# A recurrence's weights prepared in larger pieces, their transfers issued by GpSimd

## The chip, the core and the metric

The kernel runs on one core of one Trainium2 chip, in one launch. The metric is the time of one execution on the device, in microseconds (us), as the median of several runs. Engines are named as in the profile: PE is TensorE (PEld its weight loads), DVE is VectorE, ACT is ScalarE, POOL is GpSimd, SP is SyncE, which here only issues transfers (DMAs). SPq, ACTq and POOLq are these engines' own instruction queues, in which a DMA is issued or a semaphore waited for.

## What is computed

The reference takes 32 batch elements of 512 nodes with 256 channels and a 512 x 512 adjacency for each. Two layers follow each other, each with a graph part and a sequence part:

```python
x = x + gnn0(layernorm(x), adj)      # graph attention of 4 heads, relu, layernorm of each head
x = x + mamba2(layernorm(x))         # gated state-space block over the 512 nodes
x = x + gnn1(layernorm(x), adj)      # graph attention of one head, elu
x = x + lstm_part(layernorm(x))      # below
```

The last part is a recurrence that runs over the 512 nodes one after the other, for all 32 elements at once, so it can only begin when the last element has left gnn1:

```python
gates = x_proj + h @ W_hh.T                     # x_proj = x @ W_ih.T + b_ih + b_hh
i, f, g, o = split(gates, 4)
c = sigmoid(f) * c + sigmoid(i) * tanh(g)
h = sigmoid(o) * tanh(c)
```

Its hidden states are then weighted by an argmax of two logits, summed along the nodes, and combined with two vectors fw_att and bw_att. The weights of this part (W_ih, W_hh, the biases, the logit weights, fw_att, bw_att) are what the change is about. They are inputs, each used once.

## The kernel before, in words

The program has two phases. In the first, `layers_per_batch` takes the elements one after the other through gnn0, mamba2 and gnn1. Four streams of generators run at staggered times: while element b is in `mamba`, element b+2 is in gnn0 (`plain0`, then `after0`) and element b-1 is in gnn1 (`plain1`, `after1`). A loop always takes the next step of the stream whose planned time is lowest (lines 1005 to 1019); that is the order of recording. A scheduler then orders the instructions on each engine, and every engine executes its own queue strictly in order. An instruction that has to wait stops everything behind it on that engine.

A fifth stream, recorded in the last two elements (planned times from nb - 1.75 on, line 1014), is `recurrence_weights`. It reads the recurrence's weights from memory, scales and reorders their columns on GpSimd and stores the result in a DRAM tensor `wr`. The second phase, `recurrence`, begins by loading `wr` into the tile `wall` (line 1283).

The pieces of `recurrence_weights` that matter here:

- `begun` (L1078) writes a column of a tile with a copy from the current element's x. It ties the preparation to that element's place in the work. The DMA that fills the tile comes after that copy.
- The small inputs come first: eight loads for the logit weights `rwl` (L1088), the biases (L1095, L1098), and fw and bw in four loads each (L1111), with stores at L1104, L1106 and L1115.
- W_ih is taken in eight quarters of 128 x 256 (two halves k of the input channels, four quarters q): a load of the quarter into `rwraw` (L1123; two buffers, by q), a load of one row repeated on all partitions into `rwoff` (L1125), a subtraction (L1132), `ordered` (a memset of two columns, L1069, and four products, L1075) into `rwt`, and a store to `wr` (L1140). For the second half k the store has 127 rows, since the last row is another one's place (L1139).
- W_hh follows in eight quarters, each with four loads of 32 rows (L1129), `ordered`, one product of a single column (L1135) and a store.
- The pool of these tiles has one buffer for each tag. So `rwt` is used by all pieces in turn: its next memset waits until the store before has been done.
- SyncE issues all of these DMAs.

Around it, the lines that the prediction names: the store of an element's result X3 (L879, SyncE, once for each element), the broadcast loads of mamba's decay rows `bc` (L753) and `ce` (L675), of the attention's rows `rb` and `rbv` (L465), all on SyncE; `line` and `linea` to DRAM from ScalarE (L661, L452); on GpSimd the additions L494 and L605, the small pair L54/L56 (a reciprocal square root for the layer norms and for mamba's norm), the product `ce` (L746), the bias of gnn0's output `o` (L593), mamba's `xdd` (L793) and `xh` (L817). VectorE's L341 continues `o` after L593; its L783 makes `xdt`, which L793 reads, and TensorE's L780 and L800 stand before and behind it in mamba.

Of the kernel before, what the change touches and what calls it, by code (L numbers as in the profile page):

```python
# [14 lines left out]
ALU = mybir.AluOpType  # L15
# [4 lines left out]
P = 128  # L20
N = 512
NT = N // P
D = 256
DK = D // P
# [9 lines left out]
GB = 32  # L34
# [41 lines left out]
def layers_per_batch(ctx, tc, c, a, X3, odd=None, wr=None):  # L76
# [6 lines left out]
    nc = tc.nc  # L83
    nb = a.x.shape[0]
# [917 lines left out]
    def each(*parts):  # L1002
        return stream([(b + at, b + until, make, b + n) for b in range(-2, nb + 1) for at, until, make, n in parts])

    streams = [
        each((0.0, 1.0, mamba, 0)),
        each((-0.097, -0.033, mamba_in, 0), (-0.026, 0.192, mamba_dt, 0)),
        each((0.55, 0.857, second, -1), (0.857, 1.52, first, 2)),
        each((1.62, 1.75, after0, 2)),
    ]  # L1010
    if odd is not None:
        rw = ctx.enter_context(tc.tile_pool(name="rw0", bufs=1))
        now = lambda: states[int(min(at))]["x"][:, 0, 0:1]
        streams.append(nb - 1.75 + 1.5 / 64 * n for n, _ in enumerate(recurrence_weights(nc, rw, a, wr, now)))
    END = nb + 10
    at = [next(t) for t in streams]
    while min(at) < END:
        n = at.index(min(at))
        at[n] = next(streams[n], END)

    if odd is not None:
# [12 lines left out]
        for most, n in ((mall0, H0), (mall1, 1)):  # L1034
            pair = wp.tile([4 * n, n], F32, name=f"pair{n}")
# [12 lines left out]
def recurrence_weights(nc, pool, a, wr, now):  # L1048

    Q, J = 4, 64
    W = 4 * J + 2
    nw = DK * Q * W
    n0 = 2 * nw  # L1060
    half = (0.5, 0.5, 0.5, 1.0)
    order = (3, 1, 0, 2)

    def tile_(p, n, tag):
        return pool.tile([p, n], F32, tag=tag, name=tag)

    def ordered(raw, n, s):
        t = tile_(P, W, "rwt")
        nc.gpsimd.memset(t[:n, 4 * J :], 0.0)  # L1069
        halves = t[:n, : 3 * J].rearrange("p (e g j) -> p e g j", e=2, g=3)  # L1070
        for to, g in enumerate(order):
            dst, src = t[:n, 3 * J : 4 * J], raw[:n, g * J : (g + 1) * J]
            if to < 3:
                dst, src = halves[:, :, to, :], src.rearrange("p (e j) -> p e j", e=2)
            nc.gpsimd.tensor_scalar(dst, src, half[g] * s, None, ALU.mult)  # L1075
        return t

    def begun(t, *columns):  # L1078
        for n in columns or (0,):
            nc.gpsimd.tensor_copy(t[:, n : n + 1], now())  # L1080
        return t

    yield

    wl = begun(tile_(P, 2 * DK, "rwl"), 0, DK)
    for q in range(Q):
        for l in range(2):
            nc.sync.dma_start(  # L1088
                out=wl[q * 32 : (q + 1) * 32, l * DK : (l + 1) * DK],
                in_=a.wl[q : q + 1, l * J : (l + 1) * J].rearrange("o (k p) -> p (o k)", p=32),  # L1090
            )
    yield
    nc.gpsimd.tensor_tensor(wl[:, :DK], wl[:, DK:], wl[:, :DK], ALU.subtract)
    bl = begun(tile_(P, 2, "rbl"))
    nc.sync.dma_start(out=bl, in_=a.bl.to_broadcast([P, 2]))  # L1095
    b = [begun(tile_(P, 4 * J, f"rwraw{n}")) for n in range(2)]
    for t, src in zip(b, (a.bih, a.bhh)):
        nc.sync.dma_start(out=t[:Q], in_=src.rearrange("o (q r) -> (o q) r", q=Q))  # L1098
    yield
    nc.gpsimd.tensor_tensor(bl[:, 0:1], bl[:, 0:1], bl[:, 1:2], ALU.subtract)  # L1100
    nc.gpsimd.tensor_tensor(b[0][:Q], b[0][:Q], b[1][:Q], ALU.add)
    t = ordered(b[0], Q, 1.0)
    yield
    nc.sync.dma_start(out=wr[:, n0 + 2 * J : n0 + 2 * J + 1], in_=bl[:, 0:1])  # L1104
    last = wr[P - 1 : P, nw - Q * W : nw].rearrange("o (q w) -> (o q) w", q=Q)
    nc.sync.dma_start(out=last, in_=t[:Q])  # L1106
    yield
    for n, src in enumerate((a.fw, a.bw)):
        t = begun(tile_(P, W, "rwt"))
        for q in range(Q):  # L1110
            nc.sync.dma_start(out=t[q * GB : (q + 1) * GB, :J], in_=src[q : q + 1, :].to_broadcast([GB, J]))  # L1111
        yield
        nc.gpsimd.tensor_scalar(t[:, :J], t[:, :J], 0.5, None, ALU.mult)
        yield
        nc.sync.dma_start(out=wr[:, n0 + n * J : n0 + (n + 1) * J], in_=t[:, :J])  # L1115
        yield
    for n, (src, s) in enumerate(((a.wih, 1.0), (a.whh, 0.5))):
        for k in range(DK):
            for q in range(Q):
                raw = begun(tile_(P, 4 * J, f"rwraw{q % 2}"))  # L1120
                cols = slice(q * 4 * J, (q + 1) * 4 * J)
                if n == 0:
                    nc.sync.dma_start(out=raw, in_=src[k * P : (k + 1) * P, cols])  # L1123
                    off = begun(tile_(P, 4 * J, "rwoff"))
                    nc.sync.dma_start(out=off, in_=src[D - 1 : D, cols].to_broadcast([P, 4 * J]))  # L1125
                else:
                    for r in range(Q):
                        r0 = r * J + k * 32
                        nc.sync.dma_start(out=raw[r * 32 : (r + 1) * 32], in_=src[r0 : r0 + 32, cols])  # L1129
                yield  # L1130
                if n == 0:
                    nc.gpsimd.tensor_tensor(raw, raw, off, ALU.subtract)  # L1132
                t = ordered(raw, P, s)
                if n == 1:
                    nc.gpsimd.tensor_scalar(t[:, 4 * J : 4 * J + 1], wl[:, k : k + 1], 0.5, None, ALU.mult)  # L1135
                yield
                o0 = n * nw + (k * Q + q) * W

                r = P - 1 if n == 0 and k == DK - 1 else P  # L1139
                nc.sync.dma_start(out=wr[:r, o0 : o0 + W], in_=t[:r])  # L1140
                yield


def recurrence(ctx, tc, c, a, X3, wr, out):
# [247 lines left out]
@with_exitstack  # L1392
def kernel(ctx: ExitStack, tc: tile.TileContext, a, out):
    nc = tc.nc
    nb = a.x.shape[0]
    const = ctx.enter_context(tc.tile_pool(name="const", bufs=1))
    dram = ctx.enter_context(tc.tile_pool(name="dram", bufs=1, space=DRAM))
    c = setup_consts(nc, const)
    X3 = dram.tile([N, nb, D], F32, name="X3")
    wr = dram.tile([P, 2 * DK * 4 * 258 + 2 * 64 + 1], F32, name="wr")  # L1400
    odd = const.tile([1, 1], I32, name="odd")
    with ExitStack() as phase:
        layers_per_batch(phase, tc, c, a, X3, odd, wr)
    general = nc.values_load(odd, min_val=0, max_val=1, skip_runtime_bounds_check_because="it is only compared with 0")
    with tc.If(general > 0):
        with ExitStack() as phase:
            layers_per_batch(phase, tc, c, a, X3)
    with ExitStack() as phase:
        recurrence(phase, tc, c, a, X3, wr, out)
# [70 lines left out]
```

## Time and profile before

| | |
|---|---|
| median of 3 runs | 4534.08 us (4533.77 to 4534.99) |
| the profiled execution: its time | 4532.62 us |
| the profiled execution: its span | 4530.9 us |
| PE, DVE, ACT, POOL busy, of the span | 86%, 74%, 65%, 28% |
| first phase: last X3 store issued | 3211.65 us |
| second phase: `wall` loads issued | from 3220.98 us |
| DMAs issued by SyncE: packets, bytes | 269832, 271.32 MB |
| DMAs issued by GpSimd: packets, bytes | 160, 0.04 MB |
| weights: first copy on GpSimd, last store issued | 2948.65 us, 3135.90 us |

The profile is that of one execution, whose span runs from its first to its last instruction. The timelines give start and duration in us, engine, line, operation, output and input, the count (x4: four instructions in a row), and in brackets the idle time before the row with what ended it. In the table of stretches each row has the stretch and its length, then for PE, PEld, DVE, ACT and POOL the busy time and in parentheses the number of instructions, then the granted TensorE clock as a share of full speed, the busy share of the DMA engines and the GB/s moved. In the list of waits, "A <- B: total, times, longest" says that A was idle until B let it go.

### The profile page before, as it was taken

How to read it: one execution, taken by the hardware profiler on the slowest of the kernel's cores; microseconds unless marked ns; L12 is line 12 of the kernel's file. 1: busy time of each engine (PE TensorE's matmuls, PEld its weight loads, DVE VectorE, ACT ScalarE, POOL GpSimd, SP SyncE). 2: the span in 40 equal slices, each digit the busy share in tenths (PEclk: the TensorE clock that was granted, in tenths of full speed). 3: DMA queues.
4: the chain of work that ended last, by engine and by line, in shares of the span. 5: the costliest groups of instructions: out<-in, count | busy, mean ns of one | idle time of the engine just before them, and what ended most of it. 6: DMA issues, size and time to landing. Idle time of an engine off the chain costs nothing. (4 is left out here: it accounts for less than half of the span.)

```text
span 4530.9 us, 116255 instructions
## 1 busy us (share of the span) xinstructions
PE 3878.2 (86%) x46798; PEld 2389.2 (53%) x46798; DVE 3375.1 (74%) x10429; ACT 2956.8 (65%) x6852; POOL 1286.6 (28%) x1371
## 2 busy tenths in 40 slices
PE   6889999988999989998999999867688888888883
PEld 3445554455544455444555444534466666666662
DVE  4677676777667776677767677744599999999997
ACT  4677777777777777777777777755344444444441
POOL 2334433334333344333343333443000000000000
PEclk8999999999999999999999999988899999999997
DMA  3111222112221212222122211122112221222225
GB/s 107 56 61 59 75 66 73 61 64 69 72 73 61 64 57 75 71 70 64 59 71 70 73 61 64 57 68 60 52 41 46 46 46 42 45 46 46 46 41 170
DMA packets 273755, 288.69 MB, mean 64 GB/s; under 512 B 151872, under 2 KB 224536, under 8 KB 271032
## 3 DMA queue, kind: packets, MB, share of 16 engines
q1 hardware_dynamic: 269832, 271.32, 20.8%
q10 hardware_dynamic: 3216, 9.81, 0.7%
q8 instruction: 371, 6.08, 0.5%
q14 instruction: 176, 1.44, 0.1%
q0 software_dynamic: 160, 0.04, 0.0%
HBM read 227.09 MB, written 37.11 MB: 58 GB/s over the span
## 5 line engine op out<-in xcount | busy, mean ns | idle before, releaser
L1267 PE MATMUL pg<-wall,h 128*32 128x96 f32 x16352 | 558.4, 276 | 177.4 <-DVE h L1349 169.8
L1267 PEld LDWEIGHTS pg<-wall,h 128*32 128x32 f32 x16352 | 374.2, 109 | 351.0 <-DVE h L1349 332.8
L1267 PE MATMUL pg<-wall,xTr 128*32 128x96 f32 (+1 forms) x16384 | 548.3, 273 | 0.0
L484 DVE SCALAR_TENSOR_TENSOR w<-w,adjT 128x1024 f32<-128x1024 f32 x256 | 348.0, 1380 | 247.6 <-ACT w L478 247.6
L1267 PEld LDWEIGHTS pg<-wall,xTr 128*32 128x32 f32 x16384 | 447.3, 110 | 4.7 <-issue 0.3
L1326 ACT ACTIVATE z<-pg 128x96 f32<-128x96 f32 x512 | 128.7, 251 | 438.6 <-PE pg L1267 438.6
L710 DVE SCALAR_TENSOR_TENSOR acc<-px,convw,acc 128x511 f32<-128x511 f32 (+2 forms) x480 | 351.2, 743 | 83.1 <-ACT acc L705 75.3
L478 ACT ACTIVATE w<-rb,neg,colsa 128x512 f32<-128x512 f32 x512 | 387.5, 807 | 8.7 <-PE psu L556 4.4
L746 POOL TENSOR_TENSOR ce<-ce,cT 128x384 f32<-128x384 f32 x128 | 185.3, 1476 | 654.4 <-ACT cT L718 650.7
L548 PE MATMUL pav<-w,hb 128*64 128x512 f32 x1024 | 350.3, 610 | 7.4 <-DVE w L484 4.4
L1337 ACT ACTIVATE z<-z 128x32 f32<-128x32 f32 x1024 | 234.7, 229 | 168.4 <-DVE z L1335 101.0
L760 ACT ACTIVATE g<-bc,cs 128x128 f32<-128x128 f32 x1024 | 321.6, 389 | 7.3 <-DMA bc<-line 4.9
L54 POOL TENSOR_SCALAR ve<-mv 128x4 f32<-128x4 f32 x32 | 6.3, 196 | 1064.2 <-DVE mv L1191 1064.2
L689 PE MATMUL px<-mT,win 128*128 128x512 f32 x640 | 307.1, 611 | 0.0
L962 PE MATMUL pov<-wb,wv 128*128 128x257 f32 x1024 | 241.2, 388 | 72.2 <-DVE wv L484 72.2
L847 PE MATMUL po<-wc,xh 128*128 128x256 f32 x1024 | 259.4, 388 | 44.5 <-DVE xh L817 28.7
L56 POOL TENSOR_TENSOR rs<-ve,mhalf 128x4 f32<-128x4 f32 (+1 forms) x224 | 276.7, 1235 | 18.4
L962 PEld LDWEIGHTS pov<-wb,wv 128*128 128x128 f32 x1024 | 190.6, 191 | 115.8 <-DVE wv L484 87.0
L1349 DVE STREAM_TRANSPOSE h<-hh 128x32 f32<-128x32 f32 x1024 | 216.6, 212 | 34.9
L689 PE MATMUL pz<-mT,win 128*128 128x512 f32 x512 | 242.2, 606 | 0.0
L1332 DVE SCALAR_TENSOR_TENSOR ab<-z 128x64 f32<-128x64 f32 x1024 | 226.3, 221 | 14.5 <-ACT z L1326 11.2
L847 PEld LDWEIGHTS po<-wc,xh 128*128 128x128 f32 x1024 | 181.7, 192 | 88.1 <-DVE xh L817 41.3
(249 smaller groups left out, 8419.5 us busy)
## 6 DMA issues: line engine op xcount, KB each, us to landing
bc<-line SPq DMA_DIRECT2D x128, 512.0 KB, 3.6
adj<-in_adj_dram SPq DMA_DIRECT2D x32, 1024.0 KB
rb<-linea SPq DMA_DIRECT2D x64, 512.0 KB, 4.9
ce<-line SPq DMA_DIRECT2D x64, 384.0 KB, 4.5
x<-in_x_dram SPq DMA_DIRECT2D x32, 512.0 KB, 8.7
X<-x SPq DMA_DIRECT2D x32, 512.0 KB
xt<-X SPq DMA_DIRECT2D x128, 128.0 KB, 2.1
x<-X SPq DMA_DIRECT2D x128, 128.0 KB, 3.4
```

Of the source, the lines that this page charges most:

```text
L56: nc.gpsimd.tensor_tensor(rs, ve, c.mhalf[:, :n], ALU.pow)
L478: nc.scalar.activation(w[:, t, k, :], rb[:, k, :], AF.Relu, bias=neg1, scale=cols[:, 2 * m + t, h + k : h + k + 1],)
L484: nc.vector.scalar_tensor_tensor(w[:, :, k, :], w[:, :, k, :], 1.0, edges, ALU.add, ALU.mult)
L548: nc.tensor.matmul(pa[k * HO : (k + 1) * HO, :], hb[:, j, 2 * q + k, :], w[:, t, k, :], start=(j == 0), stop=(j == NT - 1),)
L689: nc.tensor.matmul(pz, win[:, k, col : col + P], mT[:, k, :], start=(k == 0), stop=(k == DK - 1))
L710: nc.vector.scalar_tensor_tensor(acc[:, s:], pz[:, : N - s], convw[:, cc, k : k + 1], acc[:, s:], ALU.mult, ALU.add)
L760: nc.scalar.activation(g[:, i, k, :], bc[:, k, i * P : (i + 1) * P], AF.Relu, bias=cs[:, i, 2 * cc + k : 2 * cc + k + 1], scale=-1.0,)
L847: nc.tensor.matmul(po[:, i * D : (i + 1) * D], xh[:, cc, it * P : (it + 1) * P], wc[:, cc, :], start=(cc == 0), stop=(cc == NC - 1),)
L962: nc.tensor.matmul(po[:, : D + 1], ws[j // 2][:, j % 2, 0, it * P : (it + 1) * P], wb[:, j, :], start=(j == 0), stop=(j == NT - 1),)
L1267: nc.tensor.matmul(p[q * GB : (q + 1) * GB, :], lhs[k], w[:, k, q, s:e], start=(start and k == 0), stop=(stop and k == DK - 1),)
L1332: nc.vector.scalar_tensor_tensor(ab, z[:, c0 + 2 * H : c0 + 4 * H], 1.0, z[:, c0 : c0 + 2 * H], ALU.add, ALU.mult)
L1337: nc.scalar.activation(z[:, (10 + n) * H : (11 + n) * H], z2[:, 4 * n * H : (4 * n + 1) * H], AF.Tanh, scale=0.5)
```

## The change

Three things change in `recurrence_weights`, and one in its pacing.

All its DMAs are issued by GpSimd, none by SyncE. `rwoff` is gone: the quarter of W_ih and the repeated row share one tile `rwraw` of 512 columns, which has a single buffer. W_ih is taken with q as the outer and k as the inner loop. W_hh is taken in four pieces of two quarters, with four loads of 32 x 512 and one store of 128 x 516 each. fw and bw share one tile, one product and one store. `ordered` takes one or two quarters; its three first products are split in two, each over 32 columns of each quarter. The planned times are spread over 48 steps where they were spread over 64 before.

```diff
--- before.py
+++ after.py
@@ -1011,7 +1011,7 @@
     if odd is not None:
         rw = ctx.enter_context(tc.tile_pool(name="rw0", bufs=1))
         now = lambda: states[int(min(at))]["x"][:, 0, 0:1]
-        streams.append(nb - 1.75 + 1.5 / 64 * n for n, _ in enumerate(recurrence_weights(nc, rw, a, wr, now)))
+        streams.append(nb - 1.75 + 1.5 / 48 * n for n, _ in enumerate(recurrence_weights(nc, rw, a, wr, now)))
     END = nb + 10
     at = [next(t) for t in streams]
     while min(at) < END:
@@ -1064,16 +1064,23 @@
     def tile_(p, n, tag):
         return pool.tile([p, n], F32, tag=tag, name=tag)
 
-    def ordered(raw, n, s):
-        t = tile_(P, W, "rwt")
-        nc.gpsimd.memset(t[:n, 4 * J :], 0.0)
-        halves = t[:n, : 3 * J].rearrange("p (e g j) -> p e g j", e=2, g=3)
+    def ordered(raw, n, quarters, s):
+
+        t = tile_(P, 2 * W, "rwt")
+        tq = t.rearrange("p (q w) -> p q w", q=2)[:n, :quarters]
+        rq = raw.rearrange("p (q w) -> p q w", q=quarters)[:n]
+        nc.gpsimd.memset(tq[:, :, 4 * J :], 0.0)
         for to, g in enumerate(order):
-            dst, src = t[:n, 3 * J : 4 * J], raw[:n, g * J : (g + 1) * J]
+            src = rq[:, :, g * J : (g + 1) * J]
             if to < 3:
-                dst, src = halves[:, :, to, :], src.rearrange("p (e j) -> p e j", e=2)
-            nc.gpsimd.tensor_scalar(dst, src, half[g] * s, None, ALU.mult)
-        return t
+                for e in range(2):
+                    nc.gpsimd.tensor_scalar(
+                        tq[:, :, (3 * e + to) * 32 : (3 * e + to + 1) * 32], src[:, :, e * 32 : (e + 1) * 32],
+                        half[g] * s, None, ALU.mult,
+                    )
+            else:
+                nc.gpsimd.tensor_scalar(tq[:, :, 3 * J : 4 * J], src, half[g] * s, None, ALU.mult)
+        return t, tq
 
     def begun(t, *columns):
         for n in columns or (0,):
@@ -1083,62 +1090,69 @@
     yield
 
     wl = begun(tile_(P, 2 * DK, "rwl"), 0, DK)
-    for q in range(Q):
-        for l in range(2):
-            nc.sync.dma_start(
+    for l in range(2):
+        for q in range(Q):
+            nc.gpsimd.dma_start(
                 out=wl[q * 32 : (q + 1) * 32, l * DK : (l + 1) * DK],
                 in_=a.wl[q : q + 1, l * J : (l + 1) * J].rearrange("o (k p) -> p (o k)", p=32),
             )
-    yield
+        yield
     nc.gpsimd.tensor_tensor(wl[:, :DK], wl[:, DK:], wl[:, :DK], ALU.subtract)
     bl = begun(tile_(P, 2, "rbl"))
-    nc.sync.dma_start(out=bl, in_=a.bl.to_broadcast([P, 2]))
-    b = [begun(tile_(P, 4 * J, f"rwraw{n}")) for n in range(2)]
+    nc.gpsimd.dma_start(out=bl, in_=a.bl.to_broadcast([P, 2]))
+    both = begun(tile_(P, 2 * 4 * J, "rwraw"), 0, 4 * J)
+    b = [both[:, : 4 * J], both[:, 4 * J :]]
     for t, src in zip(b, (a.bih, a.bhh)):
-        nc.sync.dma_start(out=t[:Q], in_=src.rearrange("o (q r) -> (o q) r", q=Q))
+        nc.gpsimd.dma_start(out=t[:Q], in_=src.rearrange("o (q r) -> (o q) r", q=Q))
     yield
     nc.gpsimd.tensor_tensor(bl[:, 0:1], bl[:, 0:1], bl[:, 1:2], ALU.subtract)
     nc.gpsimd.tensor_tensor(b[0][:Q], b[0][:Q], b[1][:Q], ALU.add)
-    t = ordered(b[0], Q, 1.0)
+    t, _ = ordered(b[0], Q, 1, 1.0)
     yield
-    nc.sync.dma_start(out=wr[:, n0 + 2 * J : n0 + 2 * J + 1], in_=bl[:, 0:1])
+    nc.gpsimd.dma_start(out=wr[:, n0 + 2 * J : n0 + 2 * J + 1], in_=bl[:, 0:1])
     last = wr[P - 1 : P, nw - Q * W : nw].rearrange("o (q w) -> (o q) w", q=Q)
-    nc.sync.dma_start(out=last, in_=t[:Q])
+    nc.gpsimd.dma_start(out=last, in_=t[:Q, :W])
     yield
+    t = begun(tile_(P, 2 * W, "rwt"))
     for n, src in enumerate((a.fw, a.bw)):
-        t = begun(tile_(P, W, "rwt"))
         for q in range(Q):
-            nc.sync.dma_start(out=t[q * GB : (q + 1) * GB, :J], in_=src[q : q + 1, :].to_broadcast([GB, J]))
-        yield
-        nc.gpsimd.tensor_scalar(t[:, :J], t[:, :J], 0.5, None, ALU.mult)
-        yield
-        nc.sync.dma_start(out=wr[:, n0 + n * J : n0 + (n + 1) * J], in_=t[:, :J])
-        yield
-    for n, (src, s) in enumerate(((a.wih, 1.0), (a.whh, 0.5))):
+            nc.gpsimd.dma_start(out=t[q * GB : (q + 1) * GB, n * J : (n + 1) * J], in_=src[q : q + 1, :].to_broadcast([GB, J]))
+        yield
+    nc.gpsimd.tensor_scalar(t[:, : 2 * J], t[:, : 2 * J], 0.5, None, ALU.mult)
+    yield
+    nc.gpsimd.dma_start(out=wr[:, n0 : n0 + 2 * J], in_=t[:, : 2 * J])
+    yield
+
+    for q in range(Q):
+        cols = slice(q * 4 * J, (q + 1) * 4 * J)
         for k in range(DK):
-            for q in range(Q):
-                raw = begun(tile_(P, 4 * J, f"rwraw{q % 2}"))
-                cols = slice(q * 4 * J, (q + 1) * 4 * J)
-                if n == 0:
-                    nc.sync.dma_start(out=raw, in_=src[k * P : (k + 1) * P, cols])
-                    off = begun(tile_(P, 4 * J, "rwoff"))
-                    nc.sync.dma_start(out=off, in_=src[D - 1 : D, cols].to_broadcast([P, 4 * J]))
-                else:
-                    for r in range(Q):
-                        r0 = r * J + k * 32
-                        nc.sync.dma_start(out=raw[r * 32 : (r + 1) * 32], in_=src[r0 : r0 + 32, cols])
-                yield
-                if n == 0:
-                    nc.gpsimd.tensor_tensor(raw, raw, off, ALU.subtract)
-                t = ordered(raw, P, s)
-                if n == 1:
-                    nc.gpsimd.tensor_scalar(t[:, 4 * J : 4 * J + 1], wl[:, k : k + 1], 0.5, None, ALU.mult)
-                yield
-                o0 = n * nw + (k * Q + q) * W
-
-                r = P - 1 if n == 0 and k == DK - 1 else P
-                nc.sync.dma_start(out=wr[:r, o0 : o0 + W], in_=t[:r])
-                yield
+            pair = begun(tile_(P, 2 * 4 * J, "rwraw"), 0, 4 * J)
+            raw, off = pair[:, : 4 * J], pair[:, 4 * J :]
+            nc.gpsimd.dma_start(out=raw, in_=a.wih[k * P : (k + 1) * P, cols])
+            nc.gpsimd.dma_start(out=off, in_=a.wih[D - 1 : D, cols].to_broadcast([P, 4 * J]))
+            yield
+            nc.gpsimd.tensor_tensor(raw, raw, off, ALU.subtract)
+            t, _ = ordered(raw, P, 1, 1.0)
+            yield
+            o0 = (k * Q + q) * W
+
+            r = P if k < DK - 1 else P - 1
+            nc.gpsimd.dma_start(out=wr[:r, o0 : o0 + W], in_=t[:r, :W])
+            yield
+    for q in (0, 2):
+        for k in range(DK):
+            raw = begun(tile_(P, 2 * 4 * J, "rwraw"))
+            for r in range(Q):
+                r0 = r * J + k * 32
+                nc.gpsimd.dma_start(out=raw[r * 32 : (r + 1) * 32], in_=a.whh[r0 : r0 + 32, q * 4 * J : (q + 2) * 4 * J])
+            yield
+            t, tq = ordered(raw, P, 2, 0.5)
+            for e in range(2):
+                nc.gpsimd.tensor_scalar(tq[:, e, 4 * J : 4 * J + 1], wl[:, k : k + 1], 0.5, None, ALU.mult)
+            yield
+            o0 = nw + (k * Q + q) * W
+            nc.gpsimd.dma_start(out=wr[:, o0 : o0 + 2 * W], in_=t)
+            yield
 
 
 def recurrence(ctx, tc, c, a, X3, wr, out):
```

In the built order five quarters of W_ih stand before L593 of the last gnn0 on GpSimd's queue, where seven stood before; three quarters and all of W_hh follow before L793 of the last `mamba`. Between the wl loads stand L494 and the second L605, and the fw and bw loads stand between the L54 and the L56 of gnn1's layer norm.

## The prediction

> **What bounds the kernel now.** I began with the stretch in which the change lives. SyncE's timeline dates the elements: each stores its result to X3 once (L879), so the distance between two such rows is one element's period.
>
> ```profile
> 2755.16 0.37 SPq L879 DMA_DIRECT2D X<-x  x1
> 2851.86 0.37 SPq L879 DMA_DIRECT2D X<-x  x1
> 2949.77 0.39 SPq L879 DMA_DIRECT2D X<-x  x1
> 3074.65 0.37 SPq L879 DMA_DIRECT2D X<-x  x1
> 3165.72 0.37 SPq L879 DMA_DIRECT2D X<-x  x1
> ```
>
> The usual period in the timeline is 95.3 us, with some of 96.7. The fourth row comes 124.9 us after the third (window 1, the first with the weights' work), 29.6 us too many. The fifth comes 91.1 us later (window 2), though no next-but-one element's first layer is left to compute there. The busy times of these stretches say who is short of work (engines in the order PE, PEld, DVE, ACT, POOL):
>
> ```profile
> 2755.20:2851.90 96.70, 87.84 (x432) 47.94 (x430) 67.60 (x140) 73.19 (x131) 37.16 (x33) 0.98 0.20 66
> 2949.80:3074.70 124.90, 85.01 (x407) 45.80 (x406) 66.00 (x128) 66.17 (x119) 54.47 (x94) 0.85 0.21 62
> 3074.70:3165.70 91.00, 69.60 (x310) 41.98 (x308) 42.05 (x91) 52.56 (x95) 33.59 (x81) 0.87 0.25 69
> ```
>
> TensorE normally works 88 of 97 us and bounds the element; in window 1 it does the same work in 125. GpSimd is the only engine with more to do, 17.3 us more, and 54 of 125 us is no full engine: it must wait. The waits of window 1 give the stall, and GpSimd's own timeline its cause:
>
> ```profile
> DVE o L341 <- POOL o L593: 30.6, 1, 30.6
> POOL rwt L1069 <- DMA wr<-rwt: 29.8, 7, 8.2
> ...
> 3014.38 0.10 POOL L1069 MEMSET rwt<- 128x2 f32 x1 [7.92 <-DMA wr<-rwt]
> 3025.05 0.10 POOL L1069 MEMSET rwt<- 128x2 f32 x1 [8.05 <-DMA wr<-rwt]
> 3035.74 0.10 POOL L1069 MEMSET rwt<- 128x2 f32 x1 [8.20 <-DMA wr<-rwt]
> 3035.81 2.48 POOL L593 TENSOR_TENSOR o<-o,bias 128x512 f32<-128x512 f32 x2
> ```
>
> Every memset of the single buffer rwt (L1069) waits until the store before has landed. The attention's bias add (L593) stands behind these in GpSimd's queue, and VectorE, then TensorE, wait for it. A usual element has L593 58.8 us after its X store (2910.66 against 2851.86); here it is 86.0 (3035.81 against 2949.77). These 27.2 us are nearly the whole 29.6: in window 1 lateness of L593 costs about one for one. The three waits of 8 us follow stores of 127 rows (L1139; SyncE issued them at 3006.24, 3016.90 and 3027.57); a store of 128 rows, issued at 3002.78, let the memset go at 3004.79, 2.0 us later.
>
> In window 2 SyncE's in-order queue is the harm. Its loads of ce and bc stand behind weight loads and stores that wait for GpSimd, and ScalarE waits:
>
> ```profile
> ACT dec L670 <- DMA wr<-rwt: 6.8, 1, 6.8
> ...
> ACT g L760 <- DMA bc<-line: 4.9, 1, 4.9
> ```
>
> TensorE loses 3.75 + 1.97 us after the first (before prv L445 and pcb L727) and 6.54 us after the second (before pxd L780).
>
> **The change, part by part.** Removed: all 87 weight DMAs leave SyncE's queue. Its 12 or so us of window 2 stalls can go; nothing then replaces them on SyncE, whose remaining rows are rb, bc, ce, rbv and X.
>
> Added on GpSimd: 66 DMA issues on an in-order engine, 37 of them ahead of L593 (8 for wl, bl, bih, bhh, 10 loads of wih, 8 for fw and bw, 8 stores), because the built order puts five of the eight wih quarters there (before: seven, and a memset behind a seventh store). 29 stand between window 2's start and L793 (6 wih loads, 16 whh loads, 7 stores). What an issue costs is the open price. The one row of it in this trace is at the kernel's end, with 32 rows of 256 B each:
>
> ```profile
> L1372 POOL DMA_DIRECT2D tots<-tot x5: 498/498/771, 4466.8 to 4469.1; - x5
> ```
>
> For the 16 issues of 32 rows ahead of L593 (and the 16 whh loads) I take 0.5 us. For the 18 with 128 rows the bounds are 0.5 (no dependence on rows: SyncE's 128-row issues take 0.33 to 0.43, no more than its 32-row ones) and 2.0 (proportional). I take 1.0, the geometric middle, an estimate, since neither end is shown. The three of 4 rows: 0.45.
>
> Sum for window 1, from GpSimd's first copy at 2948.65. Issues 18 x 1.0 + 16 x 0.5 + 3 x 0.45 = 27.4. Compute of five quarters: L1132's 0.73, six products of 32 columns (between 0.23 for one column, L1135, and 0.345 for 64, L1075: 0.295) and one of 64, 2.85 each, 14.2; bias 3.3, fw and bw once 0.55, copies and memsets 3.2, hand-overs of 0.1 before each issue and subtract about 2: 23 in all. The element's own work in between (L494, L605, two pairs L54/L56, ce L746): 11.4. Waits: rwraw is now one buffer, so each quarter waits for its load, 2.3 us after its issue (rwoff issued at 3086.35 released L1132 at 3089.55, 2.8 after its issue ended; less, as its own issue is longer now): 9; the last store 2.1, the fw/bw store and load 2. Sum 75, so L593 at 3023.5 against 3035.8: **-12.4 us**. This uses 2.1 us for each 127-row store.
>
> Here a rule of the Trainium skill decides between two sums. "DMA: Bandwidth & Descriptors", section "Why a DMA increments its semaphore by 16 and not by 1", says that 127 partitions use one DMA engine, but that on trn2 some direct copies issued from GpSimd spread even 127 over all 16. The rows (8 against 2.0 us) agree with the first half for SyncE; for GpSimd's stores no row exists. Spread, they cost what a 128-row store does and hide under the next load. On one engine the 8 us stay: two such stores lie ahead of L593, each 1.7 us beyond the load that covers it (+3.4), and two in window 2 cost +9.5. I take spread, because 127 is the number the page gives.
>
> A second rule speaks against the change: "SBUF — State Buffer", section "SBUF: two separate sides", says that GpSimd cannot write its descriptors while VectorE runs an operation in a two-port mode. The rows of window 1 show few candidates before L593: fp32 copies and tensor_scalars of 0.15 to 0.75 us. By the rule at most about 2 us are lost; by the rows nothing. I leave it at zero and in the range.
>
> Moved earlier in GpSimd's queue past other steps: eight wl issues stand before L54/L56 of ssc, which then start about 5 us later (2959.5 against 2954.4); fw/bw issues stand before the layernorm's L56 (ending at 2973.9 against 2961.6). VectorE holds its da and hb (L650, L529) behind that, about 8 us late. These do not add: L593 is later still, so they only use up slack of the same stall, until L593 would be earlier than about 3012.
>
> Window 2, from the X store: 13 issues x 1.0 + 16 x 0.5 = 21; three quarters 8.6 and four doubles (L1135 twice, memset 0.1, six of 0.345, one of 0.48) 12; copies and hand-overs 3.7; own work up to ce 12.4; waits for loads and stores 9.5: L793 at +67.2 against +65.4 before (3140.10), **+1.7 us**. So SyncE's freed 12 us buy little: GpSimd is late for xdd in its place. Behind L793 TensorE has 3.4 us of gaps, two of which go since bc and g are early: **-2**.
>
> The doubled whh pieces save products (7 for two quarters against 8) and halve stores; that is in the sums. The recurrence, its load of wall and the element loop before 2948 are the same instructions: nothing. Together -12.4 + 1.7 - 2 = about -13. The profiled execution took 4532.6 (span 4530.9), so 4519.6; the median of the three runs is 1.5 higher: **4521 us**.
>
> **The rivals.** (1) The above: 4521, own range 4513 to 4529, chance 0.42. (2) Issues cost 0.5 whatever the rows: 18 x 0.5 less in window 1, 13 x 0.5 less in window 2 (until xdt itself is last), -28: 4506. For: SyncE's flat rows. [...]0.17. (3) The 127-row stores stay on one engine: +13 on (1), 4534, no change. For: the 8 us rows. 0.19. (4) Slower: GpSimd's issuing becomes the bound. Each 0.1 us per 128-row issue costs 31 x 0.1 us over both windows, so the gain is gone at 1.4 us, and 0.2% slower comes at 1.7 (at 1.3 with (3)); at the proportional 2.0, +18: 4552. For: 66 issues on the very queue that holds up window 1 already. Against: the 0.5 us row. 0.22. That the change does not free SyncE is excluded: the built order shows no weight row left there.
>
> **How the numbers follow.** About 0.2% (9 us) is what a measurement of this kernel can tell from no change. Faster: most of (1), all of (2): 0.53. Same: the rest of (1), most of (3): 0.20. Slower: (4) and a part of (3): 0.27. The range goes from (2)'s 4505 to 4545, which leaves out some of (2) and the upper half of (4).
>
> **What would show it.** GpSimd's rows of wih loads: near 1.0 us right, 0.5 is (2), above 1.4 is (4). The L879 distances: 112 and 91 by (1). L593 near 3023, L793 near +67. Memset waits after 127-row stores: none by (1), above 1 us by (3). Wrong altogether would be a stall of TensorE that neither L593 nor L793 releases, such as VectorE held at L69 for the layernorm's L56, or SyncE's bc still late.

## The result, and the profile after

The changed kernel takes 4527.62 us (median of 20 runs, 4523.22 to 4529.83) against 4534.6 us before (20 runs beside them, 4529.36 to 4536.17): ratio 0.9984, 95% interval 0.9978 to 0.9991, so 7.0 us less. Forecast was 13.6 us less than those runs, 13 by its sum. The profiled execution took 4528.62 us (span 4526.9) against 4532.62. SyncE's timeline gives the X stores:

```profile
2756.73 0.37 SPq L879 DMA_DIRECT2D X<-x  x1
2853.42 0.37 SPq L879 DMA_DIRECT2D X<-x  x1
2948.98 0.37 SPq L879 DMA_DIRECT2D X<-x  x1
3065.28 0.37 SPq L879 DMA_DIRECT2D X<-x  x1
3162.11 0.37 SPq L879 DMA_DIRECT2D X<-x  x1
```

Window 1 is 116.3 us long (124.9 before), window 2 is 96.8 (91.1 before). One correction to how I read the kernel before: there the store that opens window 1 was itself 2.3 us late. VectorE's L878 had finished x at 2947.45, but the store left at 2949.77, behind rwl loads that waited for GpSimd; after the change the two are 2948.96 and 2948.98. So window 1 is judged together with the period in front of it: 222.8 us before, 211.9 after, **-10.9**. Window 2 gives **+5.7**, the last stretch (45.9, now 45.3) -0.6. The sum is -5.8; from the store near 2087 to the last one the profiles show 1125.0 and 1119.0, -6.0. (The two profiled executions differ by 4.0 only, since the changed one had reached that store 1.7 us later, 2088.40 against 2086.66.)

The table of stretches (columns as before) shows where GpSimd's time goes; its count includes the DMA issues, its busy time does too:

```profile
2949.00:3065.30 116.30, 89.59 (x422) 48.52 (x420) 65.19 (x128) 68.36 (x123) 72.33 (x138) 0.90 0.22 60
3065.30:3162.10 96.80, 72.23 (x309) 43.10 (x307) 42.45 (x91) 52.71 (x95) 54.66 (x123) 0.82 0.26 73
```

GpSimd is busy 17.9 and 21.1 us more. Its DMA issues alone take 20.7 us ahead of L593, where its compute fell with the quarters, and 15.9 us ahead of L793. The waits of window 1, and below them those of window 2:

```profile
POOL rwraw L1134 <- DMA rwraw<-in_wih_dram: 13.6, 4, 4.5
DVE o L341 <- POOL o L593: 12.7, 1, 12.7
```

```profile
PE pst L800 <- POOL xdd L793: 10.4, 1, 10.4
POOL rwt L1072 <- DMA wr<-rwt: 6.8, 2, 5.8
```

L593 still holds up VectorE, 12.7 us where it was 30.6. The 8 us waits for stores are gone, and waits for loads stand in their place. In window 2 ScalarE's waits for dec and bc are gone from the list (dec L670 waits 0.51 us instead of 6.84), and TensorE now waits 10.4 us for xdd. GpSimd's timeline shows the price of an issue and what a 127-row store from GpSimd does (all three L1140 here have 127 rows):

```profile
2992.73 0.59 POOL L1140 DMA_DIRECT2D wr<-rwt  x1 [0.30 <-POOL rwt L1082]
2993.82 0.58 POOL L1131 DMA_DIRECT2D rwraw<-in_wih_dram  x1 [0.18 <-POOL rwraw L1087]
2995.03 0.10 POOL L1072 MEMSET rwt<- 128x2 f32 x1
...
3010.76 0.60 POOL L1140 DMA_DIRECT2D wr<-rwt  x1 [0.30 <-POOL rwt L1082]
...
3016.82 0.12 POOL L1072 MEMSET rwt<- 128x2 f32 x1
...
3096.30 0.61 POOL L1140 DMA_DIRECT2D wr<-rwt  x1 [0.30 <-POOL rwt L1082]
3105.20 0.10 POOL L1072 MEMSET rwt<- 128x4 f32 x1 [5.80 <-DMA wr<-rwt]
```

The memsets behind the first two of these stores have waited for nothing, the first of them 2.3 us after the issue. Issues take 0.5 to 0.66 us, with 128 rows or 32. The last pair is the exception, to which I come back: 8.9 us from issue to memset.

### The profile page after: what moved, and what is told of

It is laid out like the page before. It is cut to its first block, busy times and chain, and to the rows that moved or that the text cites. A ratio compares the mean times of both kernels' runs of the same rounds, so it can differ in the third digit from the quotient of the medians.

```text
span 4526.9 us, 116183 instructions
## 1 busy us (share of the span) xinstructions
PE 3887.8 (86%) x46798; PEld 2396.5 (53%) x46798; DVE 3373.9 (75%) x10429; ACT 2954.9 (65%) x6852; POOL 1321.7 (29%) x1450
## 3 DMA queue, kind: packets, MB, share of 16 engines
q1 hardware_dynamic: 262128, 265.91, 20.7%
## 5 line engine op out<-in xcount | busy, mean ns | idle before, releaser
L54 POOL TENSOR_SCALAR ve<-mv 128x4 f32<-128x4 f32 x32 | 6.2, 193 | 1063.8 <-DVE mv L1205 1063.8
L56 POOL TENSOR_TENSOR rs<-ve,mhalf 128x4 f32<-128x4 f32 (+1 forms) x224 | 276.6, 1235 | 18.4
L962 PEld LDWEIGHTS pov<-wb,wv 128*128 128x128 f32 x1024 | 190.4, 191 | 113.8 <-DVE wv L484 86.3
```

Of the source, the lines that this page charges most:

```text
L56: nc.gpsimd.tensor_tensor(rs, ve, c.mhalf[:, :n], ALU.pow)
L962: nc.tensor.matmul(po[:, : D + 1], ws[j // 2][:, j % 2, 0, it * P : (it + 1) * P], wb[:, j, :], start=(j == 0), stop=(j == NT - 1),)
```

## The experiments

I had two theories of the 7 us. **A**: GpSimd's queue in front of L593 and L793 sets both windows, and the gain is that 127-row stores from GpSimd no longer crawl through one DMA engine. **B**: the gain belongs to the larger pieces and to the slower pace, which put five quarters ahead of L593 instead of seven; who issues is of no account.

All times are medians; each ratio is against runs of the kernel before on the same chip, whose median lay between 4534.29 and 4535.47 us. From the L879 rows of each profile, in us: the period ahead of window 1 and window 1 together, window 2, the last stretch.

| kernel | time | ratio (95% interval) | to and with window 1 | window 2 | last |
|---|---|---|---|---|---|
| before | 4534.6 | 1 | 222.8 | 91.1 | 45.9 |
| changed | 4527.62 | 0.9984 (0.9978 to 0.9991) | 211.9 | 96.8 | 45.3 |
| e1 changed, SyncE issues | 4523.07 | 0.9973 (0.9964 to 0.9982) | 210.4 | 95.7 | 45.2 |
| e2 before, GpSimd issues | 4531.98 | 0.9994 (0.9986 to 1.0002) | 220.2 | 91.9 | 45.4 |
| e3 before, 128-row stores | 4514.35 | 0.9955 (0.9942 to 0.9969) | 210.2 | 85.4 | 45.5 |
| e4 changed, eight elements | 4569.22 | 1.0073 (1.0059 to 1.0087) | 209.0 | 76.6 | 43.6 |
| e5 changed, 128-row stores | 4527.39 | 0.9981 (0.9974 to 0.9988) | 210.5 | 95.8 | 43.7 |
| e6 no preparation | 4492.31 | 0.9905 (0.989 to 0.992) | 192.2 | 76.8 | 45.1 |
| e7 tied to dec, GpSimd | 4487.03 | 0.9893 (0.9878 to 0.9908) | 192.2 | 76.8 | 43.7 |
| e8 tied to dec, SyncE | 4485.67 | 0.9894 (0.9879 to 0.9909) | 192.2 | 76.9 | 43.6 |
| e9 before, tied to dec | 4505.36 | 0.9934 (0.992 to 0.9947) | 192.2 | 76.7 | 43.6 |
| e10 before, loops exchanged | 4534.23 | 0.9999 (0.9991 to 1.0008) | 222.8 | 91.5 | 46.9 |
| e11 before, slower pace | 4530.35 | 0.999 (0.9984 to 0.9997) | 214.1 | 99.5 | 43.5 |

**e1 and e2: the two halves of the change, each alone.** e1 is the changed kernel with SyncE issuing, e2 the kernel before with GpSimd issuing; in each, every weight DMA is edited in this way (e2 the other way round):

```diff
-            nc.gpsimd.dma_start(out=raw, in_=a.wih[k * P : (k + 1) * P, cols])
+            nc.sync.dma_start(out=raw, in_=a.wih[k * P : (k + 1) * P, cols])
```

> The changed kernel with every weight DMA issued by SyncE again; pieces, buffers, order of loops and pacing stay as changed. Theory A (what bounds windows 1 and 2 is GpSimd's queue ahead of L593 and of L793; the gain came from 127-row stores that no longer hold one DMA engine): the memset waits after 127-row stores are 6 to 8 us again, two of them ahead of L593; against that GpSimd is rid of some 21 us of issuing there, so L593 comes about 68 us after the X store (changed kernel 76.8), and in window 2 SyncE's late ce and bc come back in part. Time 4515 to 4528. Theory B (the gain is that of the larger pieces and the fewer quarters ahead of L593, whoever issues): no long memset waits, window 1 of 116 us and 4527 within 3 us.

> The kernel before with only the issuing engine changed: small pieces, eight wih and eight whh quarters, all 87 weight DMAs issued by GpSimd. Theory A: the 8 us memset waits fall to about 2 us (three in window 1, 18 us less), but some 45 issues of 0.55 us stand ahead of L593, 25 us more, and 45 ahead of L793: L593 88 to 95 us after the X store, time 4535 to 4550. Theory B: the issuer does not matter, 4534 within 3 us.

e1 has the whole gain and some 5 us more; e2's interval holds no change. So the gain comes with the pieces and the pace, as B has it, and not with the issuer. But neither theory holds whole. e1's time lies in A's range (4515 to 4528) and 1 us under B's, and the long waits that B excluded are there, one ahead of L593 and two in window 2 (6.53 us, and the second row here); e2's time lies in B's range and not in A's. GpSimd's timeline in e1:

```profile
3018.04 0.10 POOL L1072 MEMSET rwt<- 128x2 f32 x1 [7.75 <-DMA wr<-rwt]
...
3100.54 0.10 POOL L1072 MEMSET rwt<- 128x4 f32 x1 [8.03 <-DMA wr<-rwt]
```

L593 comes 74.3 us after the X store, not 68 as A expected, and 75.4 us after GpSimd's first copy, where the changed kernel has 75.6: GpSimd is rid of 20.7 us of issues, but waits 38.7 us for transfers and for cT where the changed kernel waits 19.3.

In e2 no memset ahead of L593 waits over 2.1 us, so A's saving is there too. It is paid back at once: 44 issues ahead of L593 take 24.8 us of GpSimd, and L593 comes at +86.3 from the X store:

```profile
3035.97 0.10 POOL L1069 MEMSET rwt<- 128x2 f32 x1 [1.71 <-DMA wr<-rwt]
3036.03 2.48 POOL L593 TENSOR_TENSOR o<-o,bias 128x512 f32<-128x512 f32 x2
```

So the spread stores save about what their issuing costs. Between the changed kernel and e1 lie 4.6 us, 2.7 of them in the three columns of the table, but from two comparisons whose intervals overlap; that GpSimd's issuing makes this change slower is likely, not settled.

**e3: what the 127 rows cost before.** The kernel before with 128 rows in every store. It leaves the summed biases out of the result, since the last row overwrites them.

```diff
-                r = P - 1 if n == 0 and k == DK - 1 else P
+                r = P
```

> The kernel before with one number changed: the stores of the second half of W_ih have 128 rows and not 127 (the summed biases' row is overwritten, so the biases are left out). Theory A: each of the three 8 us waits ahead of L593 falls to about 2 us, L593 comes 18 us earlier (about 68 us after the X store), window 1 takes about 107 us, and one such wait less in window 2; time 4508 to 4518. Theory B: the stores are not what holds GpSimd, since loads and SyncE's queue are behind them; time within 4 us of 4534.

20 us less, nearly three times the gain of the whole change, with 12.6 us to and with window 1 (A expected 18) and 5.7 in window 2. The 8 us rows cost the kernel before these 20 us, as A has it; what A misses is the price at which GpSimd buys them back.

**e4: the same pieces over eight elements.** The idea was that a fifth of the work would fit into each element's idle time.

```diff
-        streams.append(nb - 1.75 + 1.5 / 48 * n for n, _ in ...)
+        streams.append(nb - 8 + 7.5 / 48 * n for n, _ in ...)
```

> The changed kernel with its 48 steps spread over the last eight elements and not the last two (planned from nb - 8 on, 7.5/48 of an element each). Theory A: no element has more than two pieces on GpSimd between its other work, which GpSimd's idle time of some 60 us in each element hides: windows of 95 to 97 us up to the end, the last full one 86 us, time 4495 to 4506. Theory B (each piece costs what it costs wherever it stands): some 2 to 3 us in each of eight elements, time 4518 to 4528.

It missed by far: 34 us slower. Six elements become 10 to 18 us longer each (105.8 to 113.8 us), and only the stretches of the table gain. GpSimd's timeline of one element, whose X store was at 2488.12, shows why:

```profile
2486.94 2.30 POOL L605 TENSOR_TENSOR x<-x,blin 128x512 f32<-128x512 f32 x1 [2.04 <-ACT xm L71]
2489.30 0.31 POOL L1087 COPY rwraw<-x 128x1 f32<-128x1 f32 x2
2489.78 0.65 POOL L1131 DMA_DIRECT2D rwraw<-in_wih_dram  x1 [0.17 <-POOL rwraw L1087]
...
2506.53 0.65 POOL L1140 DMA_DIRECT2D wr<-rwt  x1 [0.30 <-POOL rwt L1082]
2511.26 0.10 POOL L1072 MEMSET rwt<- 128x2 f32 x1 [4.08 <-DMA wr<-rwt]
2511.45 0.18 POOL L54 TENSOR_SCALAR ve<-bnmv 128x4 f32<-128x4 f32 x1
...
2540.85 5.86 POOL L746 TENSOR_TENSOR ce<-ce,cT 128x384 f32<-128x384 f32 x4 [24.28 <-ACT cT L718]
2560.66 2.49 POOL L593 TENSOR_TENSOR o<-o,bias 128x512 f32<-128x512 f32 x2 [13.95 <-DVE o L586]
```

The pieces don't follow their planned times. `begun` copies from x; as soon as x is ready, right after the X store, the element's pieces stand at the head of GpSimd's queue, ahead of the L54/L56 pairs of the layer norm for which VectorE waits (the L54 at 2511.45 is 23.3 us behind the X store; the like one before stands at 12.8):

```profile
DVE x L865 <- POOL rs L56: 7.1, 1, 7.1
DVE off L69 <- POOL rs L56: 5.8, 3, 4.6
```

In an element of the kernel before without weights these two are 1.4 and 2.2 us. After that GpSimd idles for 24 and 14 us, as it does in such an element (21 and 14). So the place of the work is paid for, while there would be idle time enough for its amount. Theory A was too narrow: ahead of L593 and L793 is only one place of this kind.

**e5: is the last wait in the changed kernel one of 127 rows?** The changed kernel, all stores with 128 rows, the biases left out as in e3.

> The changed kernel, with its four 127-row stores made 128 rows (this leaves the summed biases out of the result). Theory C: GpSimd's 127-row stores are spread like 128-row ones, and the 5.8 us that a memset waited after the last of them came from transfers that SyncE had queued at the same moment; then nothing changes: 4524 to 4531 us, ratio to the kernel before 0.9975 to 0.9992, and that memset still waits 4 us or more. Rival D: some of the 127-row stores do still go to one engine; then that wait falls under 1 us and the time to about 4520.

The time does not change (C). The wait is 3.4 us instead of 5.8, under C's 4 and far over D's 1:

```profile
3096.12 0.61 POOL L1140 DMA_DIRECT2D wr<-rwt  x1 [0.30 <-POOL rwt L1082]
3102.63 0.10 POOL L1072 MEMSET rwt<- 128x4 f32 x1 [3.39 <-DMA wr<-rwt]
```

What stands there is a collision. In the changed kernel SyncE, now free, issues bc, both halves of ce and bc again at 3093.12 to 3095.24, when GpSimd's store comes. The view of DMAs between 3096 and 3106 has the mean share of the engines in 40 slices, and then the issues with the median us to landing:

```profile
DMA  3345668979999999999998998999986644100001
...
rwraw<-in_whh_dram POOLq DMA_DIRECT2D x4, 64.0 KB, 7.7
wr<-rwt POOLq DMA_DIRECT2D x1, 128.0 KB, 8.9
```

For some 5 us the 16 engines are busy for 80% or more on average. In e5 the same loads left 1.0 to 1.5 us earlier (3091.66 to 3094.22), GpSimd's store only 0.2, and it landed after 6.5 us instead of 8.9. That fits a collision, but how much of the 2.4 us the 128th row has, e5 can't say. That SyncE's loads left at that moment because their line was free is read from the timeline; no other run moved them apart.

**e6: the price of the preparation.** Five plain copies from the weights to `wr` take its place, so `wr` holds unordered weights.

> The changed kernel without the preparation: five plain copies from the weights to wr take its place, so that wr holds unordered weights. It is the price of the whole preparation. If the stall of L593 and the lateness of L793 are all that it costs, the distances of the X stores become 95 to 97, about 76 and about 45 us (76.6 was seen where only a fifth of the pieces was left in the last stretch), 44 us less than before in all: 4487 to 4494 us. If TensorE or VectorE lose time in these stretches for another reason, 4500 or more.

Windows of 95.2 and 76.8 us: against e6 the three columns of the table are 45.7 us longer before and 39.9 longer after the change. The change had removed an eighth of what the preparation costs. The copies are tied to no tile, and GpSimd issues them 7 to 24 us after the start, so these stretches hold no weights' work at all.

**e7, e8, e9: another place.** If the place decides, the pieces should be tied to a tile that is ready when GpSimd has nothing to do. mamba's `dec` (L670) is ready behind the last L56, ahead of ce.

```diff
-        now = lambda: states[int(min(at))]["x"][:, 0, 0:1]
-        streams.append(nb - 1.75 + 1.5 / 48 * n for n, _ in ...)
+        now = lambda: states[int(min(at))]["dec"][:, 0, 0, 0:1]
+        streams.append(nb - 8 + n // 6 + 0.25 + 0.12 * (n % 6) for n, _ in ...)
```

> The changed kernel with its pieces tied to mamba's dec tile instead of x, six steps in each of the last eight elements, so that GpSimd takes them in its idle 21 us before ce (L746) and 14 us before L593. Theory A': the preparation costs time only where it stands in front of a waited-for GpSimd instruction (after the X store: L54 to L56; later: L593, L793). Then nearly all of it is hidden: X store distances 95 to 97 throughout, L593 at +58 to +60, 4488 to 4498 us. Rival: the pieces cost by their amount wherever they are (contention of transfers[...]): as with the eight-element spread tied to x, 10 us and more for each element, above 4540 us.

> The same as the kernel tied to dec, but SyncE issues the weight transfers. GpSimd then has no issue time, but SyncE's loads of ce and bc stand behind weight transfers that wait for GpSimd, and the 127-row stores take 8 us. If GpSimd's issue time is what matters: as fast as with GpSimd or 1 to 5 us faster, 4486 to 4494. If SyncE's queue matters: L760 and the ce product wait, 3 to 5 us in several of the eight elements, 4500 to 4525.

Both have the windows of e6, to 0.1 us: the preparation is hidden, and the time is 4487.03 and 4485.67 us, 48 to 50 us below the kernel before and 40 to 42 below the change. Their intervals are nearly the same, so who issues makes no difference here; e8's rival, SyncE's late ce and bc, did not come true. (e6 is slower than both by what lies ahead of its first X store, which comes at 277.66, that of e7 at 272.62: its copies put 2.18 MB among the kernel's first loads, and the 5 us stay to the end. That the one causes the other is read from the traces; no run tested it.) The spread over eight elements and the tie were changed together; e4 shows that the spread alone does harm, and the tie alone was not run. GpSimd's timeline in e7:

```profile
2486.88 1.01 POOL L56 TENSOR_TENSOR rs<-ve,mhalf 128x4 f32<-128x4 f32 x1
2496.28 0.30 POOL L1087 COPY rwraw<-dec 128x1 f32<-128x1 f32 x2 [8.40 <-ACT dec L670]
...
2507.55 0.09 POOL L1072 MEMSET rwt<- 128x2 f32 x1 [1.53 <-DMA wr<-rwt]
2509.03 5.85 POOL L746 TENSOR_TENSOR ce<-ce,cT 128x384 f32<-128x384 f32 x4 [1.38 <-ACT cT L718]
2528.83 2.50 POOL L593 TENSOR_TENSOR o<-o,bias 128x512 f32<-128x512 f32 x2 [13.95 <-DVE o L586]
```

The piece starts 8.4 us behind the last L56 and ends before cT is there; L593 waits for VectorE as in an element without weights. e9 does the same to the kernel before, small pieces and SyncE's issuing included, with eight steps an element (`nb - 8 + n // 8 + 0.25 + 0.09 * (n % 8)`).

> The kernel before (small pieces, SyncE issuing), with only the tie changed from x to dec and eight steps in each of the last eight elements. Theory A': where the pieces stand on GpSimd decides, neither their size nor who issues: 4484 to 4492 us, like the two tied kernels. Rival: the larger pieces are needed too, because the small ones bring more 8 us waits per element than the idle 21 + 14 us hold: then L593 is late in several elements and the time is 4495 to 4515.

29 us less, so its rival came true and not A': windows 1 and 2 are as in e6, but two elements on the way last 101.6 and 105.9 us. There one and two waits of 8 us for 127-row stores stand ahead of L593, in a gap that is already full; VectorE waits 4.9 and 9.2 us for L593. The one of the first:

```profile
2629.70 0.10 POOL L1069 MEMSET rwt<- 128x2 f32 x1 [8.20 <-DMA wr<-rwt]
2629.76 2.49 POOL L593 TENSOR_TENSOR o<-o,bias 128x512 f32<-128x512 f32 x2
```

So the place is worth most, and the changed pieces, with their loops and their six steps an element, another 18 to 20 us once the place is right.

**e10 and e11: what in the larger pieces acts.** e10 exchanges the loops of the kernel before, as the change does for W_ih; e11 only slows its pace.

```diff
-        for k in range(DK):
-            for q in range(Q):
-                raw = begun(tile_(P, 4 * J, f"rwraw{q % 2}"))
+        for k, q in [(k, q) for q in range(Q) for k in range(DK)]:
+            if True:
+                raw = begun(tile_(P, 4 * J, f"rwraw{k}"))
```

```diff
-        streams.append(nb - 1.75 + 1.5 / 64 * n for n, _ in ...)
+        streams.append(nb - 1.75 + 1.5 / 56 * n for n, _ in ...)
```

> The kernel before, with W_ih taken in the order of the changed kernel (q outer, k inner), nothing else. The 127-row stores are then every second one instead of the last four, and the first of the three ahead of L593 can be hidden by ce. Theory B1: the order of the stores explains most of the 12 us of the changed kernel with SyncE issuing: one 8 us wait fewer ahead of L593, 4525 to 4529 us. Rival B2: it is the quarters moved behind L593, and this order changes nothing: 4533 to 4536.

> The kernel before with 1.5/56 a step in place of 1.5/64, which puts six quarters ahead of L593 instead of seven; one quarter, with its 127-row store, moves to the next stretch. Theory B2: the first stretch falls by 10 to 11 us, and the next grows by less, since L793 there still waits 4.2 us for xdt after GpSimd is done: +4 to +7; 4528 to 4531 us. Rival: the moved quarter costs the next stretch as much as it saved: 4533 to 4537.

The loops do nothing (B1 fails: all three 127-row waits still show, 7.20, 6.20 and 8.06 us). One quarter moved behind L593 takes 8.7 us from the stretch to window 1 and gives window 2 8.4 back; 2.4 come from the last stretch. That is more than the 4 to 7 I expected window 2 to pay, so the time fell into B2's range with the help of the last stretch, and by itself the slower pace mostly moves the stall. e1 moves two quarters, takes off 12.4 and gives back only 4.6. What else e1 changes must make the difference: the doubled W_hh pieces, the joined tile of W_ih, or the loops at this pace, which e10 tried at the old pace only. Which of them, no run separates.

## Why the prediction was right, and where it was not

- **Direction and size.** 13 us forecast, 7.0 measured, inside the case's own range (4513 to 4529), 1.4 us from its upper end. The second window holds most of the miss; the signs "112 and 91" came as 116.3 and 96.8.
- **Window 1, -12.4.** Measured -10.9, and L593 came 75.6 us after GpSimd's first copy where the sum said 75. But two of its terms were wrong and cancelled, so that the sum came out was luck. From GpSimd's rows between first copy and L593: 37 issues take 20.7 us (27.4 forecast), the element's own work 10.2 (11.4), the preparation's compute 22.0 with 3.1 of hand-overs to its own DMAs (23 forecast for both), waits for DMAs 19.3 (13).
- **The price of an issue**, 1.0 us for 128 rows, was the term most wrong: 0.54 to 0.66. The middle between two far ends was taken where the one row, 0.5 us, lay on one end; the likeliest value was the row. Rival (2) had this price, and its 4506 did not come: the 6.7 us saved on issues ahead of L593 went into 6.2 more of waits for DMAs.
- **Waits for loads**: 2.3 us after the issue was too little even in a quiet moment. The row that it came from says 2.8, and window 2's three loads of W_ih took 2.8 to 3.1; those behind which GpSimd waited in window 1 took 3.1 to 4.7. Four of them held GpSimd for 13.6 us in all, the longest for 4.5, as SyncE's bc and ce were issued beside it.
- **127-row stores spread**: right. Three of the four left the memset no wait, in e5 128 rows change nothing, and the rule that I used from the Trainium skill, "DMA: Bandwidth & Descriptors", section "Why a DMA increments its semaphore by 16 and not by 1", agrees with this case on both sides: from issue to memset 8.1 to 8.2 us behind SyncE's three stores ahead of L593 before, 2.3 behind GpSimd's. With such a store of SyncE alone on its way (3011 to 3014 in the kernel before) the engines moved 20 to 21 GB/s; GpSimd's at 2992.73 went mostly at 110 to 275. Rival (3) is out.
- **DVE holding up GpSimd's descriptors**, the second rule, set to zero: no run here shows it at work, and no issue of a weight DMA in the trace is longer than 0.77 us.
- **Window 2, +1.7 and -2**: this step failed. It was +5.7, and -0.6 in the last stretch. L793 came at +71.4 from the X store (+67.2 forecast): issues only 15.9 us (21 forecast), compute and hand-overs 26.1 (24.3), the element's own work 10.1 (12.4), but waits for DMAs 15.0 (9.5) and 6.6 more for other engines, which I had not put in (these rows overlap by some 2 us). The largest wait is the collision of e5, 5.8 us. The 2 us behind L793 never came: from L793 to the X store it is 25.4 us, before 25.6.
- **SyncE's freed 12 us buy little**: right. TensorE's stalls for dec and bc are gone; one of 10.4 us for xdd replaced them, and the freed transfers took part in it.
- **Why it gains.** I gave the credit of window 1 to the 8 us waits and five quarters for seven together, with the issues as the price. e1 and e2 show that the first only pays for the issues, and that the gain is pieces and pace.

## What to carry to other kernels

Side work on an engine with slack costs by its place in that engine's queue, as long as the idle time there holds its amount: look where it stands, ahead of which instruction that others wait for, and tie it to a tile that is ready when the engine falls idle. Here that was worth 29 us with the old pieces and 40 to 42 more than the change with the new ones, on either issuer, where the change itself won 7. A queue that is made free will start its transfers earlier, and what they then meet belongs in the sum.

## What was not expected of the hardware

- An issue from GpSimd cost 0.50 to 0.66 us in nearly every row, for 4, 32 or 128 rows; a DMA that follows GpSimd's own compute waited another 0.17 to 0.30 us for it.
- A 128 KB store from GpSimd landed 2.3 us after its issue when alone, and 8.9 us after it when SyncE had queued bc and ce at the same time.
